# A two-layer metaformer block: area attention with more of its second channel half in the prologue, its last result by halves, and its variance two steps earlier

## The chip, the cores and the metric

The kernel runs on one core of one Trainium2 chip. A core has five engines, each with a queue of its own that it works off in order: TensorE (PE in the profile, with its weight loads as PEld), VectorE (DVE), ScalarE (ACT), GpSimd (POOL) and SyncE (SP, which here only issues DMA). The metric is the device time of one launch in microseconds (us).

## The reference, cut to what matters

Two layers work on x of shape (2, 256, 64, 64). The first layer adds area attention and then an LSTM over tokens; the second adds a mixer with a state-space part and then a layer of experts. The change touches only the area attention:

```python
x = x + _L0_conv_ref(_ln_c(x), ...)      # _ln_c: normalise over the 256 channels
# in _L0_conv_ref, after batch norms folded into scales:
qk, vv = 1x1 projections of the normalised x
pp = 5x5 depthwise convolution of vv, padded by 2
# 8 areas: 2 images x 4 bands of 16 rows (1024 positions each); 8 heads of 32
attn = softmax(q . k / sqrt(32))          # inside one area
o = attn . v
return 1x1 projection of (o + pp)
```

All of it is computed in float32.

## The kernel before, in words

The function `area_attention` (line 94) runs 16 groups, two for each of the 8 areas: group G is area A = G // 2 and channel half c = G % 2, that is four heads. A group has 16 steps. Step t takes query half n = t // 8 (512 queries) and key block m = t % 8 (128 keys). The loop over all 256 steps stands at the end of the function. The order of instructions on each engine is the order in which the source issues them (`manual_schedule`), and the tables in the source say which piece of side work is issued in which step.

One step issues, in this order:

- `scores` (line 347): for each head a small bf16 matmul that puts the negated row maxima into PSUM (line 352) and the float32 matmul of key and query on top (line 357); then ACT makes the exponentials (line 364) into two tiles `ex`. There are three buffers of each `ex` tile for even m, one for odd m.
- `values` (line 374) of the step before: weights times V, summed over the 8 steps in the bank `av_o` (line 370).
- work from a table SMALL: `place` (line 290) turns the row maxima of a later half on PE (line 294), copies them on ACT (line 298, `rows`) and spreads them with four small DMAs on SP (line 301).
- `maxima` (line 265): the scores of a later group, transposed in role (line 270), and DVE's maximum over them (line 275). This is how the row maxima of the softmax are known before its exponentials.
- one addition of two `ex` tiles on POOL (line 577), a part of the softmax's sums. A dependency written by hand ties it to the DVE operation before the maxima and to the last matmul of the maxima, so that it runs beside the reductions.
- a number of taps of the convolution on DVE (line 324), from the tables TAPS and TAPS_FIRST; an area has 50, the two first ones of line 313 included.
- work from the tables MINE/FIRST and AROUND: projections (`query`, `key`, `v_half`, `output`, all through line 166), averages over channels (`mean`, `variance`, line 178) and transposes of V (`v_tokens`, line 239). Most of them use the one PSUM bank `po`, which ACT empties.
- `sums` (line 385) two steps after each fourth step: the sums on PE, then after every second half DVE's division (lines 397 to 405).
- work from LATE and LATE_AROUND: `join` (line 280, row maxima in three bf16 parts), `centre` (line 187), `square`, `root` (lines 199 to 206: a transpose on DVE, an addition and a power on POOL, a transpose back on DVE), `scale`, `add_taps` (line 332), `residual` (line 345).

`scores` and `maxima` share the PSUM tiles `ps` of two banks each; there are three of them, so that a tile can be written when the one three places before it was emptied. There is one buffer `xn` of normalised x.

An entry `(k, f, ...)` in MINE means f for group G + k; in AROUND it means f for area A + k. So `(1, variance, 0)` in AROUND[0] at step 6 is the variance of the next area, first half, in step 6 of every even group. Area 0 has tables of its own, for both of its groups.

Before the loop stands a prologue for area 0: mean, centring, variance, root and scaling by halves (the generator `norm`), then query, key, eight `maxima`, V, `join` and `place`. After the loop: the last additions, the last `sums`, `add_taps` and the output of the last area in four projections, each of 512 positions by 128 channels, and two residual additions of 1024 positions.

The next stage, the LSTM's `recurrence`, starts with small loads of weights for the mixers (`bc_rest`, `taps`, `w_xdt`, `w_dtp`, `w_in`), a copy `w_dt` on DVE (line 1120), and transposes of x on PE (line 693).

Of the kernel before, what the change touches and what calls it, by code (L numbers as in the profile page):

```python
# [18 lines left out]
P = 128  # L19
# [74 lines left out]
def area_attention(tc, sh, ap):  # L94
# [13 lines left out]
    with ExitStack() as ctx:  # L108
# [42 lines left out]
        def bank():  # L151
            return ps2.tile([P, 512], F32, name="po", tag="po")
# [78 lines left out]
        def v_tokens(A, c, half):  # L231

            blocks = bank().rearrange("p (m d) -> p m d", d=P)
            src = vhs[A][:, c, 2 : 2 + AROWS].rearrange("p r w -> p (r w)")
            if half == 0:
                vts[A, c] = p2.tile([P, NM, P], F32, name="vt")
            for m in range(HM):
                at = (half * HM + m) * P
                nc.tensor.transpose(blocks[:, m], src[:, at : at + P], sh.ident)
            nc.scalar.copy(vts[A, c][:, half * HM : half * HM + HM], blocks)  # L240

        def rows_of(wt, G, half, name, s, t):
            A, c = GROUPS[G]
            ps = bank()
            project(wt, c, columns(xns[A]), half, ps)
            out = p2.tile([P, 512], F32, name=f"{name}{half}")
            nc.scalar.activation(out, ps, AF.Identity, scale=s[:, c : c + 1], bias=t[:, c : c + 1])
            return out

        def query(G, half):  # L250
            if half == 0:
                nms[G] = p3.tile([P, NQ, GH, NM], F32, name="nm")
            qs[G, half] = rows_of(w["wq"], G, half, "q", s_qk, t_qk)

        def key(G, half):
            ks[G, half] = rows_of(w["wk"], G, half, "k", s_qk[:, 2:4], t_qk[:, 2:4])

        def head(h):
            return slice(HD * h, HD * h + HD)
# [149 lines left out]
        with ExitStack() as own:  # L409
            early[0] = own.enter_context(tc.tile_pool(name="a_early", bufs=1))  # L410
            def fold(name, k):
                cols = sh.prm[:, COL[name]].rearrange("p (f k) -> p f k", k=k)
                return bn_fold(nc, cp, sh.eps5, *(cols[:, f] for f in range(4)), name)

            s_qk, t_qk = fold("qk", 4)
            s_v, t_v = fold("v", 2)
            for half in range(2):
                mean(0, half)

            def norm(at, half):  # L420
                for c in range(2):
                    centre(0, c, at)
                    square(0, c, at)
                yield
                variance(0, half)
                yield
                root(0, 0, at)
                root(0, 1, at)
                yield
                for c in range(2):  # L430
                    scale(0, c, at)
                yield

            first, second = (norm(at, half) for half, at in enumerate(HALVES))
            next(first)
            next(first)
            next(second)
            for _ in first:
                pass
            query(0, 0)  # L440
            key(0, 0)
            next(second)
            maxima(0, 0)
            next(second)
            maxima(0, 1)
            next(second)
            maxima(0, 2)
            key(0, 1)
            maxima(0, 3)
            s_pe, t_pe = fold("pe", 2)  # L450
            s_pr, t_pr = fold("pr", 2)

            nc.scalar.activation(p1.tile([P, 1], F32, name="idle"), sh.eps5, AF.Exp)

            w_pe = cp.tile([P, 2, 25], F32, name="w_pe")
            for c in range(2):
                every = sh.prm[:, COL["w_pe"]].rearrange("p (c k) -> p c k", c=2)
                nc.vector.tensor_scalar(w_pe[:, c], every[:, c], s_pe[:, c : c + 1], None, ALU.mult)
            for at, works in enumerate([
                [(0, 0), (0, 1)], [(1, 0)], [(1, 1)], [],  # L460
            ]):
                maxima(0, at + 4)
                for c, half in works:
                    v_half(0, c, half)
            join(0, 0, nc.vector)
            place(0, 0)
            for half in range(2):
                v_tokens(0, 0, half)
            early[0] = None
        pe = ctx.enter_context(tc.tile_pool(name="a_ex", bufs=1))  # L470

# [5 lines left out]
        LATE = {5: [(1, join, 0)], 13: [(1, join, 1)]}  # L477
        AROUND = [
            {
                2: [(0, v_tokens, 1, 0)], 3: [(0, v_tokens, 1, 1)], 4: [(-1, output, 0, 0)],  # L480
                6: [(1, variance, 0)], 7: [(1, variance, 1)], 8: [(-1, output, 0, 1)],
                10: [(-1, output, 1, 0)], 14: [(1, v_half, 0, 0)],
            },
            {
# [5 lines left out]
        LATE_AROUND = [  # L490
            {
                0: [(1, centre, 0)], 1: [(1, square, 0)], 2: [(1, centre, 1), (-1, add_taps, 1)],
                3: [(1, square, 1)], 7: [(1, root, 0)],
                8: [(1, root, 1), (1, scale, 0)], 9: [(-1, residual, 0)], 10: [(1, scale, 1)],
            },
            {7: [(-1, residual, 1)], 15: [(0, add_taps, 0)]},
        ]

        FIRST = [
            {  # L500
                0: [(0, query, 1)], 1: [(1, query, 0)], 2: [(1, key, 0)], 3: [(1, key, 1)],
                4: [(1, query, 1)], 14: [(2, query, 0)], 15: [(2, key, 0)],
            },
            {0: [(1, key, 1)], 2: [(1, query, 1)], 11: [(2, query, 0)], 12: [(2, key, 0)], 15: [(2, key, 1)]},
        ]
        SMALL_FIRST = [{5: [(0, place, 1)], 13: [(1, place, 0)]}, SMALL]
        LATE_FIRST = [{4: [(0, join, 1)], 9: [(1, join, 0)], 13: [(1, join, 1)]}, LATE]
        AROUND_FIRST = [
            {
                6: [(1, mean, 0)], 7: [(1, mean, 1)], 8: [(0, v_tokens, 1, 0)], 10: [(1, variance, 0)],  # L510
                11: [(1, variance, 1)], 12: [(0, v_tokens, 1, 1)],
            },
            {
                1: [(1, v_half, 0, 0)], 3: [(1, v_half, 1, 0)], 4: [(1, v_half, 0, 1)], 6: [(1, v_half, 1, 1)],
                7: [(1, v_tokens, 0, 0)], 8: [(1, v_tokens, 0, 1)], 10: [(2, mean, 0)], 14: [(2, mean, 1)],
            },
        ]
        LATE_AROUND_FIRST = [
            {
                7: [(1, centre, 0)], 8: [(1, centre, 1), (1, square, 0)], 9: [(1, square, 1)],  # L520
                11: [(1, root, 0)], 12: [(1, root, 1), (1, scale, 0)], 13: [(1, scale, 1)],
            },
            LATE_AROUND[1],
        ]


        AHEAD = {t: [(1, t + 2)] if t < 14 else [(2, t - 14)] for t in range(16)}
        order = [(0, 8 + i) for i in range(8)] + [(1, i) for i in range(16)]
        AHEAD_FIRST = [{}, {**AHEAD, 0: [(1, 0), (1, 1)], 1: [(1, 2), (1, 3)]}]
        for t in range(1, 14):  # L530
            AHEAD_FIRST[0][t] = [order.pop(0) for _ in range(2 if t < 12 else 1)]

        TAPS = [
            [1, 0, 0, 2, 2, 2, 2, 1, 0, 0, 1, 2, 2, 2, 3, 2],
            [2, 0, 2, 2, 3, 2, 2, 1, 1, 0, 3, 2, 3, 2, 2, 1],
        ]
        TAPS_FIRST = [
            [3] + [0] * 11 + [2, 2, 4, 4],
            [1, 1, 3, 2, 2, 2, 3, 2, 2, 2, 2, 3, 3, 2, 3, 2],
        ]  # L540

        def works(G, t, *tables):
# [12 lines left out]
        for g in range(16 * len(GROUPS)):  # L555
            G, t = divmod(g, 16)
            A, c = GROUPS[G]
            n, m = divmod(t, NM)
            new = A == 0
            if t == 0 and c == 0:  # L560
                conv = taps(A)
            exs = scores(G, n, m)
            if pending is not None:
                values(*pending)
            works(G, t, SMALL_FIRST[c] if new else SMALL, {})

            mm, before = None, latest[0]
            for k, at in (AHEAD_FIRST[c] if new else AHEAD).get(t, ()):
                if G + k < len(GROUPS):
                    mm = maxima(G + k, at)  # L570
            pair = None
# [4 lines left out]
            if pair is not None:  # L576
                add = nc.gpsimd.tensor_tensor(pair[0], *pair, ALU.add)  # L577
                if mm is not None:
                    tc.add_manual_dep(add.ins, mm.name, at_end, reason="beside the reductions")
                    tc.add_manual_dep(add.ins, before.name, at_end, reason="beside the reductions")  # L580
            for _ in range((TAPS_FIRST if new else TAPS)[c][t]):
                next(conv, None)
            works(G, t, FIRST[c] if new else MINE, (AROUND_FIRST if new else AROUND)[c])
            if g in due:
                sums(*due.pop(g))
            works(G, t, LATE_FIRST[c] if new else LATE, (LATE_AROUND_FIRST if new else LATE_AROUND)[c])
            pending = G, n, m, exs
            if m % 2:
                odd = exs[1]
                if m % 4 == 3:  # L590
                    due[g + 2] = G, n, m // 4, pairs
                    pairs = pairs[-1:]
            else:
                pairs = (pairs if m % 4 else []) + [exs]
        nc.gpsimd.tensor_tensor(pairs[-1][1], pairs[-1][1], odd, ALU.add)
        values(*pending)
        for g in sorted(due):
            sums(*due[g])
        last = len(AREAS) - 1
        add_taps(last, 1)  # L600
        for co in range(2):
            for half in range(2):
                output(last, co, half)
            residual(last, co)


def root_steps(nc, pool, v, shape, eps, name="ir"):
# [1655 lines left out]
```

## Time and profile before

| what | us |
|---|---|
| median of 3 runs (lowest, highest) | 3035.14 (3035.07, 3035.3) |
| the profiled execution | 3031.56 |
| its span, first to last instruction | 3029.7 |
| prologue of attention, to the loop's first bias matmul | 69.85 |
| groups 0 and 1 (area 0) | 114.33, 106.04 |
| groups 2 to 13 | 1056.20 |
| groups 14 and 15 and what follows, to the last residual addition | 184.55 |
| all later stages | 1498.73 |
| PE busy in the span | 2738.2 (90%) |
| DVE busy | 2181.1 (72%) |
| ACT busy | 1347.7 (44%) |
| POOL busy | 1358.4 (45%) |

The stretches are cut by time: a group begins with the first matmul of line 352 in its first step. Lines of the profile name the engine, the source line, the operation, the tile written and the tiles read, the size, the number of instructions merged in the row, and in square brackets the idle time before them and what ended it. Row times are start and length in us from the span's start. A projection of 128 x 512 in float32 shows as four matmul passes.

### The profile page before, as it was taken

How to read it: one execution, taken by the hardware profiler on the slowest of the kernel's cores; microseconds unless marked ns; L12 is line 12 of the kernel's file. 1: busy time of each engine (PE TensorE's matmuls, PEld its weight loads, DVE VectorE, ACT ScalarE, POOL GpSimd, SP SyncE). 2: the span in 40 equal slices, each digit the busy share in tenths (PEclk: the TensorE clock that was granted, in tenths of full speed). 3: DMA queues.
4: the chain of work that ended last, by engine and by line, in shares of the span. 5: the costliest groups of instructions: out<-in, count | busy, mean ns of one | idle time of the engine just before them, and what ended most of it. 6: DMA issues, size and time to landing. Idle time of an engine off the chain costs nothing. (4 is left out here: it accounts for less than half of the span.)

```text
span 3029.7 us, 45443 instructions
## 1 busy us (share of the span) xinstructions
PE 2738.2 (90%) x17798; PEld 1519.2 (50%) x17798; DVE 2181.1 (72%) x3224; ACT 1347.7 (44%) x2417; POOL 1358.4 (45%) x1037
## 2 busy tenths in 40 slices
PE   6989999999999999998789999978887589999994
PEld 2222232332323233222179999963444478888882
DVE  4689999999989999898956676679988812222115
ACT  2334454554544454444444455557653822222223
POOL 1354545544454554545623000028773156666651
PEclk8999999999999999999889999989999789999995
DMA  3000000000000000000024000005552446666658
GB/s 126 1 1 1 1 1 1 1 1 1 1 1 1 1 1 1 2 1 1 5 87 161 2 1 1 2 12 153 146 145 64 159 164 228 227 226 227 227 189 337
DMA packets 58658, 220.33 MB, mean 73 GB/s; under 512 B 14440, under 2 KB 15344, under 8 KB 48704
## 3 DMA queue, kind: packets, MB, share of 16 engines
q0 software_dynamic: 25440, 125.24, 11.6%
q1 hardware_dynamic: 31760, 87.82, 9.0%
q10 hardware_dynamic: 1232, 4.25, 0.4%
q8 instruction: 142, 2.33, 0.3%
q14 instruction: 84, 0.69, 0.1%
HBM read 173.30 MB, written 43.58 MB: 72 GB/s over the span
## 5 line engine op out<-in xcount | busy, mean ns | idle before, releaser
L577 POOL TENSOR_TENSOR ex<-ex,ex 128x1024 f32<-128x1024 f32 x255 | 614.5, 2412 | 645.3 <-PE ps L270 287.5
L275 DVE TENSOR_REDUCE nm<-ps 128x2 f32<-128x1024 f32 x512 | 601.0, 1218 | 102.4 <-PE ps L270 101.6
L364 ACT ACTIVATE ex<-ps 128x1024 f32<-128x1024 f32 x512 | 497.9, 1022 | 308.2 <-PE ps L357 269.3
L324 DVE SCALAR_TENSOR_TENSOR acc<-vh,w_pe,acc 128x1008 f32<-128x1008 f32 (+7 forms) x384 | 553.0, 1442 | 7.1
L270 PE MATMUL ps<-k,q 32*128 32x512 f32 x2048 | 347.7, 644 | 13.1 <-DVE nm L275 13.1
L2007 DVE COPY xt<-px 128x512 f32<-128x512 f32 x68 | 47.0, 691 | 397.7 <-PE px L2005 397.7
L2019 ACT ACTIVATE act<-ph,wt 128x256 f32<-128x256 f32 x272 | 128.8, 474 | 396.0 <-PE ph L2017 391.9
L2017 PE MATMUL ph<-xt,wt 128*128 128x256 f32 x1088 | 293.2, 393 | 3.3 <-ACT act L2019 1.7
L357 PE MATMUL ps<-q,k 32*128 32x512 f32 x2048 | 285.0, 607 | 0.0
L370 PE MATMUL av_o<-ex,vt 128*32 128x512 f32 x2048 | 278.0, 609 | 4.8 <-ACT ex L364 4.6
L2027 PE MATMUL py<-wt,act 128*128 128x256 f32 x1088 | 279.6, 380 | 0.0
L270 PEld LDWEIGHTS ps<-k,q 32*128 32x128 f32 x2048 | 123.1, 184 | 216.1 <-issue 75.0
L2017 PEld LDWEIGHTS ph<-xt,wt 128*128 128x128 f32 x1088 | 191.6, 192 | 66.4 <-DVE xt L2007 23.4
L774 PE MATMUL z<-xs,u 128*128 128x128 f32 x1872 | 222.2, 275 | 0.4 <-ACT xs L754 0.4
L774 PEld LDWEIGHTS z<-xs,u 128*128 128x128 f32 x1872 | 215.7, 192 | 0.6 <-ACT xs L754 0.6
L2027 PEld LDWEIGHTS py<-wt,act 128*128 128x128 f32 x1088 | 202.2, 191 | 25.0
L798 ACT ACTIVATE t<-z,bias 128x128 f32<-128x128 f32 x468 | 136.3, 361 | 144.5 <-PE z L786 144.4
L2042 POOL DMA_INDIRECT results<-y,ri x136 | 138.0, 1015 | 139.4 <-DVE y L2035 98.3
L786 PE MATMUL z<-xs,v 128*128 128x128 f32 x1512 | 180.1, 275 | 0.1
L786 PEld LDWEIGHTS z<-xs,v 128*128 128x128 f32 x1512 | 174.3, 192 | 0.7 <-DVE xs L805 0.7
L1508 POOL TENSOR_TENSOR cs<-hs,cs 128x1024 f32<-128x1024 f32 x63 | 148.7, 2363 | 54.1 <-DVE hs L1501 32.7
L370 PE MATMUL po<-ex,ones 128*32 128x512 f32 x1024 | 136.6, 638 | 37.0 <-ACT rows L298 25.7
(408 smaller groups left out, 3809.9 us busy)
## 6 DMA issues: line engine op xcount, KB each, us to landing
cs<-c_rows SPq DMA_DIRECT2D x128, 256.0 KB
y<-results SPq DMA_DIRECT2D x32, 512.0 KB
x<-xrows SPq DMA_DIRECT2D x8, 1024.0 KB
rows<-xt SPq DMA_DIRECT2D x16, 512.0 KB
out_x<-res POOLq DMA_DIRECT2D x15, 512.0 KB, 7.1
xrows<-xn SPq DMA_DIRECT2D x24, 256.0 KB
x<-in_x SPq DMA_DIRECT2D x4, 1024.0 KB
x<-in_x ACTq DMA_DIRECT2D x4, 1024.0 KB
```

What stands on the lines that cost most here:

```text
L270: mm = nc.tensor.matmul(tiles[h // 2][:, h % 2], qs[G, i // HM][head(h), i % HM * P : (i % HM + 1) * P], ks[G, n][head(h)], start=True, st ...
L275: nc.vector.tensor_reduce(nms[G][:, n, 2 * j : 2 * j + 2, i], tiles[j], AX.X, ALU.max, negate=True)
L324: mark(nc.vector.scalar_tensor_tensor(part, vh[:, c, 2 + r0 + dy : 2 + r1 + dy, w0 + dx : w1 + dx], w_pe[:, c, k : k + 1], part, ALU.mult, ...
L357: nc.tensor.matmul(tiles[h // 2][:, h % 2], k[head(h), m % HM * P : (m % HM + 1) * P], qs[G, n][head(h)], start=False, stop=True, tile_pos ...
L364: nc.scalar.activation(exs[i], tiles[i], AF.Exp, scale=HD**-0.5)
L370: nc.tensor.matmul(to[head(h)], lhs, exs[h // 2][:, h % 2], start=first, stop=last, tile_position=(0, HD * h))
L577: add = nc.gpsimd.tensor_tensor(pair[0], *pair, ALU.add)
L774: nc.tensor.matmul(z[c][:, g, :m], u[:, k, c, g], xt[:, k], start=g == GATES[0] and k == 0, stop=False, skip_group_check=True,)
L786: nc.tensor.matmul(z[c][:, g, :m], v[:, k, c, g], h[:, k], start=False, stop=k == 1, skip_group_check=True,)
L1508: nc.gpsimd.tensor_tensor(now["c", n], hs, now["c", n], ALU.mult)
L2017: nc.tensor.matmul(ph[:, hc], wt[:, at : at + P], xt[:, c], start=c == 0, stop=c == 1)
L2027: nc.tensor.matmul(py[:, j], act[:, hc, j * P : j * P + P], wt[:, at : at + C], start=hc == 0, stop=hc == NH - 1,)
```

## The change

Five things are done.

1. In the prologue, area 1's mean is issued after the first variance; query(0,0) and key(0,0) go into `ps` tiles instead of the bank `po`; the second root part is issued one piece later. query(0,1), query(1,0) and key(1,0) are issued before the loop.
2. Group 0 has tables of its own; group 1 uses the general ones. Steps 0 to 9 of group 0 hold two `maxima`, steps 10 to 15 one; group 1 has one in every step. Area 0's taps are 13 in group 0 and 37 in group 1 (before 15 and 35).
3. In even groups, the next area's variance is issued in steps 4 and 6 (before 6 and 7), the first root part in step 6 (before 7), and the previous area's first output half in step 7 (before 4).
4. After the loop, the last area's output is made by halves of 512 positions: the half of y that is complete is added to the convolution, projected and added to x before the last `sums` are issued; then the other half. Both projections of a half use the two banks of one `ps` tile.
5. `rows_of`, `query` and `key` take the PSUM tile as an argument.

```diff
-        def rows_of(wt, G, half, name, s, t):
+        def rows_of(wt, G, half, name, s, t, ps):
             A, c = GROUPS[G]
-            ps = bank()
+            ps = bank() if ps is None else ps
...
             next(first)
             next(first)
             next(second)
+
+            for half in range(2):
+                mean(1, half)
             for _ in first:
                 pass
-            query(0, 0)
-            key(0, 0)
+            query(0, 0, wide()[:, 0])
+            key(0, 0, wide()[:, 0])
             next(second)
             maxima(0, 0)
             next(second)
             maxima(0, 1)
-            next(second)
             maxima(0, 2)
+            for _ in second:
+                pass
+            maxima(0, 3)
             key(0, 1)
-            maxima(0, 3)
...
-            for at, works in enumerate([
-                [(0, 0), (0, 1)], [(1, 0)], [(1, 1)], [],
-            ]):
+            for at in range(4):
                 maxima(0, at + 4)
-                for c, half in works:
-                    v_half(0, c, half)
+                v_half(0, *divmod(at, 2))
+            for half in range(2):
+                v_tokens(0, 0, half)
+            query(0, 1, wide()[:, 0])
             join(0, 0, nc.vector)
             place(0, 0)
-            for half in range(2):
-                v_tokens(0, 0, half)
+            query(1, 0, wide()[:, 0])
+            key(1, 0, wide()[:, 0])
...
         AROUND = [
             {
-                2: [(0, v_tokens, 1, 0)], 3: [(0, v_tokens, 1, 1)], 4: [(-1, output, 0, 0)],
-                6: [(1, variance, 0)], 7: [(1, variance, 1)], 8: [(-1, output, 0, 1)],
+                2: [(0, v_tokens, 1, 0)], 3: [(0, v_tokens, 1, 1)], 4: [(1, variance, 0)],
+                6: [(1, variance, 1)], 7: [(-1, output, 0, 0)], 8: [(-1, output, 0, 1)],
...
-                3: [(1, square, 1)], 7: [(1, root, 0)],
+                3: [(1, square, 1)], 6: [(1, root, 0)],
...
+        FIRST = {
+            0: [(1, key, 1)], 1: [(1, query, 1)], 11: [(2, query, 0)], 12: [(2, key, 0)], 15: [(2, key, 1)],
+        }
+        SMALL_FIRST = {5: [(0, place, 1)], 9: [(1, place, 0)]}
+        LATE_FIRST = {3: [(0, join, 1)], 7: [(1, join, 0)], 13: [(1, join, 1)]}
+        LATE_AROUND_FIRST = {
+            1: [(1, centre, 0)], 2: [(1, centre, 1), (1, square, 0)], 3: [(1, square, 1)],
+            6: [(1, root, 0)], 8: [(1, root, 1), (1, scale, 0)], 9: [(1, scale, 1)],
+        }
...
-        AHEAD_FIRST = [{}, {**AHEAD, 0: [(1, 0), (1, 1)], 1: [(1, 2), (1, 3)]}]
-        for t in range(1, 14):
-            AHEAD_FIRST[0][t] = [order.pop(0) for _ in range(2 if t < 12 else 1)]
+        AHEAD_FIRST = dict(AHEAD)
+        for t in range(14):
+            AHEAD_FIRST[t] = [order.pop(0) for _ in range(2 if t < 10 else 1)]
...
         TAPS_FIRST = [
-            [3] + [0] * 11 + [2, 2, 4, 4],
-            [1, 1, 3, 2, 2, 2, 3, 2, 2, 2, 2, 3, 3, 2, 3, 2],
+            [0] * 10 + [1, 2, 3, 2, 3, 2],
+            [2, 0, 2, 2, 3, 3, 3, 2, 2, 0, 3, 3, 3, 3, 3, 3],
         ]
...
-            new = A == 0
+            new = G == 0
...
-        for g in sorted(due):
-            sums(*due[g])
         last = len(AREAS) - 1
-        add_taps(last, 1)
-        for co in range(2):
-            for half in range(2):
-                output(last, co, half)
-            residual(last, co)
+        acc = accs.pop((last, 1)).rearrange("p r w -> p (r w)")
+        for half, at in enumerate(HALVES):
+            if half == 1:
+                for g in sorted(due):
+                    sums(*due[g])
+            y = ys[last, 1][:, at]
+            nc.vector.tensor_tensor(y, y, acc[:, at], ALU.add)
+            ps = wide()
+            for co in range(2):
+                project(w["wpr"], co, lambda k: ys[last, k], half, ps[:, co])
+                o = p2.tile([P, 512], F32, name="o_last", tag=f"q{half}")
+                nc.scalar.activation(
+                    o, ps[:, co], AF.Identity, scale=s_pr[:, co : co + 1], bias=t_pr[:, co : co + 1]
+                )
+                to = area(last)[:, co, at]
+                nc.vector.tensor_tensor(to, to, o, ALU.add)
```

More of the change, by code (lines that the diff above doesn't have):

```diff
@@ L248, in rows_of, with query, key @@
             return out
-        def query(G, half):
+        def query(G, half, ps=None):
             if half == 0:
                 nms[G] = p3.tile([P, NQ, GH, NM], F32, name="nm")
-            qs[G, half] = rows_of(w["wq"], G, half, "q", s_qk, t_qk)
-        def key(G, half):
-            ks[G, half] = rows_of(w["wk"], G, half, "k", s_qk[:, 2:4], t_qk[:, 2:4])
+            qs[G, half] = rows_of(w["wq"], G, half, "q", s_qk, t_qk, ps)
+        def key(G, half, ps=None):
+            ks[G, half] = rows_of(w["wk"], G, half, "k", s_qk[:, 2:4], t_qk[:, 2:4], ps)
         def head(h):
@@ L427, in norm @@
                 root(0, 0, at)
+                yield
                 root(0, 1, at)
-                yield
                 for c in range(2):
@@ L497, in area_attention @@
         ]
[L499 to L524, printed above, removed]
+        FIRST = {
[7 more added lines that the diff above has]
+        }
         AHEAD = {t: [(1, t + 2)] if t < 14 else [(2, t - 14)] for t in range(16)}
         order = [(0, 8 + i) for i in range(8)] + [(1, i) for i in range(16)]
-        AHEAD_FIRST = [{}, {**AHEAD, 0: [(1, 0), (1, 1)], 1: [(1, 2), (1, 3)]}]
-        for t in range(1, 14):
-            AHEAD_FIRST[0][t] = [order.pop(0) for _ in range(2 if t < 12 else 1)]
+        AHEAD_FIRST = dict(AHEAD)
+        for t in range(14):
+            AHEAD_FIRST[t] = [order.pop(0) for _ in range(2 if t < 10 else 1)]
         TAPS = [
@@ L564, in area_attention @@
                 values(*pending)
-            works(G, t, SMALL_FIRST[c] if new else SMALL, {})
+            works(G, t, SMALL_FIRST if new else SMALL, {})
             mm, before = None, latest[0]
-            for k, at in (AHEAD_FIRST[c] if new else AHEAD).get(t, ()):
+            for k, at in (AHEAD_FIRST if new else AHEAD).get(t, ()):
                 if G + k < len(GROUPS):
@@ L580, in area_attention @@
                     tc.add_manual_dep(add.ins, before.name, at_end, reason="beside the reductions")
-            for _ in range((TAPS_FIRST if new else TAPS)[c][t]):
+            for _ in range((TAPS_FIRST if A == 0 else TAPS)[c][t]):
                 next(conv, None)
-            works(G, t, FIRST[c] if new else MINE, (AROUND_FIRST if new else AROUND)[c])
+            works(G, t, FIRST if new else MINE, AROUND[c])
             if g in due:
                 sums(*due.pop(g))
-            works(G, t, LATE_FIRST[c] if new else LATE, (LATE_AROUND_FIRST if new else LATE_AROUND)[c])
+            works(G, t, LATE_FIRST if new else LATE, LATE_AROUND_FIRST if new else LATE_AROUND[c])
             pending = G, n, m, exs
```

## The prediction

> **What bounds the kernel now.** I read the busy time by stage first (stretches cut at the first bias matmul, line 352, of each step or group), then the instructions in order of time at the places that the diff touches. The page's chain of waits lies almost wholly in the last stage and says nothing here. Stretches of the attention stage, each as start:end, length, then busy time of PE, PEld, DVE, ACT, POOL with counts, clock, DMA share, GB/s: the prologue, groups 0 and 1, an even group (4), an odd one (3), and the end.
>
> ```profile
> 0.00:69.85 69.85, 42.63 (x118) 14.31 (x119) 33.05 (x57) 14.34 (x24) 10.71 (x18) 0.86 0.36 136
> 69.85:184.18 114.33, 107.71 (x607) 33.24 (x606) 77.44 (x70) 42.79 (x51) 44.76 (x29) 0.95 0.01 1
> 184.18:290.22 106.04, 95.89 (x584) 29.69 (x584) 96.27 (x84) 43.57 (x52) 43.61 (x29) 0.94 0.00 1
> 382.08:467.93 85.85, 84.39 (x564) 26.64 (x564) 83.12 (x75) 42.00 (x50) 41.59 (x27) 1.00 0.01 2
> 467.93:557.98 90.05, 85.65 (x565) 26.77 (x565) 81.75 (x75) 44.01 (x52) 47.59 (x29) 0.98 0.00 1
> 1489.78:1530.97 41.19, 23.43 (x66) 6.52 (x62) 24.32 (x29) 6.69 (x9) 7.63 (x5) 0.67 0.03 8
> ```
>
> The steady groups have PE and DVE both nearly full (84.4 and 83.1 of 85.85), so a gain there can only be a stall that goes. The slack is in the prologue and the end, and even groups are some 4 to 5 us longer than odd ones. Group 4 shows why (in order of time):
>
> ```profile
> 513.23 5.46 POOL L203 TENSOR_TENSOR root<-root,minus_half 128x32 f32<-128x32 f32 x1
> 518.65 2.34 POOL L577 TENSOR_TENSOR ex<-ex,ex 128x1024 f32<-128x1024 f32 x1
> 521.03 1.02 ACT L364 ACTIVATE ex<-ps 128x1024 f32<-128x1024 f32 x1 [3.50 <-POOL ex L577]
> 522.25 3.31 PE L370 MATMUL po<-ex,ones 128*32 128x512 f32 x16 [3.54 <-ACT rows L298]
> ```
>
> POOL's power holds its queue 5.46 us; step 8's pair addition comes late; step 9's second exponential waits for that (the odd `ex` tile has one buffer); behind it on ACT stands `rows` of `place`; PE's sums need the one `po` bank that `rows` empties. Step 9 takes 10.35 us (515.15 to 525.50) instead of the 6.07 of group 3.
>
> **Prologue: gain 9.3.** The projections in it are latency-bound and cold:
>
> ```profile
> 22.08 3.75 PE L166 MATMUL po<-xn,wq 128*128 128x512 f32 x4 [6.35 <-issue]
> 26.70 3.69 PE L166 MATMUL po<-xn,wk 128*128 128x512 f32 x4 [0.87 <-ACT q L247]
> 31.26 1.98 PE L178 MATMUL po<-sq,mean_w 128*128 128x512 f32 x4 [0.87 <-ACT k L247]
> ```
>
> Area 1's mean (2 x 1.98, two copies of 0.58) goes into PE's idle 15.7 to 22.1; area 1's x is there by 11.7 (its bytes in the DMA record). The Trainium skill ("TensorE: Matmul & The Clock Gate", Part 1) says that about 3.4 us of activity releases the clock and an idle window of that length throttles it. The row agrees for the idle 6.35 (3.75 for what takes 1.98 warm). With the gaps down to about 1 us the rule gives 1.98 each for query and key; if they stayed cold, as in the row, the sum loses 3.5. I take warm. Key no longer waits for query's copy, being in another bank: query 22.1-24.0, key 24.0-25.7, copy 26.5, variance 25.5-27.3, first reduction 28.5 (now 34.35). DVE then does 2 reductions, a transpose 31.6, 4 reductions to 36.3 (POOL's root hides under these; before, DVE idled for it from 37.3 to 40.8), transpose and two scalings 38.3, 2 reductions 40.6. PE: second key 37.7-39.5, copy 40.4, then four rounds of maxima and `v_half`, PE-bound at 3.0 each, to 52.4; vh copy 53.2; two token transposes with copies 55.7; query(0,1) to 56.9; `place`; rows on ACT at 58.0, behind q's copy. Before, rows ended at 67.28 and line 357 began at 71.62, 4.3 later, waiting for the four small DMAs on SP; so now 62.3. query(1,0) and key(1,0), 3.8 of PE, fit into these 4.3.
>
> **Groups 0 and 1: gain 15.7.** Five projections (area 1's mean twice, query(0,1), query(1,0), key(1,0)) leave the loop, and 10 steps instead of 13 hold two maxima; the `mx` loads on SP are as many as before and queue behind nothing. A step with two maxima and a projection stays 7.61 (three PSUM buffers, which ACT and DVE must empty; its plain PE work is 6.6), with transposes 6.3, with neither 5.7. Step 0 ends at 62.3 + 5.4 + 1.9 = 69.6. Steps 1 to 9: 7.6 + 6.3 + 6.9 + 8.1 + 7.7 + 7.6 + 5.7 + 6.5 + 8.5 = 64.9; centring (1.2 twice) waits for query(1,1), the last reader of the one `xn` buffer, and costs about 0.6 in steps 3 and 4; the power ends in bare steps 7 to 8, where POOL has room. That is 134.5. From there DVE bounds. A tap costs 1.32: group 1's 96.27 less 18 pairs of reductions at 2.36, two sum ends of 3.03 and 1.5 of small work, over 35. Steps 10 to 15: 6 x 2.36 + 13 x 1.32 + 0.2 = 31.5; group 1, now 16 pairs and 37 taps: 37.8 + 48.8 + 6.1 + 1.5 = 94.2; 1 carried over. 126.7 at 97% busy (group 3's share) is 130.6, so group 2 begins at 265.1, not 290.2: 25.1 with the prologue.
>
> **Even groups 2 to 12: gain 2.4 each, 14.4.** Variance moves to steps 4 and 6 (squares end 489.3, its matmul at 491.8: no wait), output(-1,0,0) from 4 to 7; PE's work is the same. But `ln_t` cannot move a whole step: on DVE it stands behind step 6's two taps, which end at 507.99, so it runs 508.0-509.2 (before 511.5-512.7), power 509.8-515.2. Queued behind `ln_t` are step 7's reductions (1.3 later): PE waits 0.55 for a PSUM tile at step 8. Behind the power are now two additions, 515.2-517.6 and 517.6-519.9. Step 9 starts at 515.7; its second exponential 519.95, rows 521.2 (before 522.2), sums 521.25-523.2, warm after 1.5 idle, where they took 3.31. So step 9 ends at 523.2 against 525.5, and step 11 sheds 0.1. DVE's wait for the root (3.2) goes, but is off the path. Bounds: 0 if the additions come no earlier, 4.6 if even groups reach the odd ones' length. Group 14 has no variance; its output in step 7 fills a PE idle of 2.6: gain 1 (0 to 2).
>
> **The end: loss 3.6.** What is there now:
>
> ```profile
> 1505.59 1.22 DVE L332 TENSOR_TENSOR y<-y,acc 128x1024 f32<-128x1024 f32 x1
> 1506.60 0.27 SPq L1117 DMA_DIRECT2D w_dtp<-in_w_dtp  x1
> ...
> 1525.27 3.63 PE L166 MATMUL po<-y,wpr 128*128 128x512 f32 x4 [0.87 <-ACT o L339]
> 1529.75 1.22 DVE L345 TENSOR_TENSOR x<-x,o 128x1024 f32<-128x1024 f32 x1 [7.93 <-ACT o L339]
> 1531.51 2.89 PE L693 MATMUL turned<-ident,x 128*128 128x128 f32 x13 [2.61 <-DVE w_dt L1120]
> ```
>
> After: half 0's addition ends at 1507.5, co 0 projected by 1510.5, copied 1511.3. The second projection waits for this copy although it goes into another bank: both are one `wide` tile and the built program has the wait. co 1 to 1515.2; only then, in PE's order, the sums, to 1517.6; DVE's sum end and half addition, 3.9, to 1521.5; then projection, copy, projection, copy, addition: 1526.8 if PE is warm, 1529.5 if cold, against 1530.97. The same skill rule speaks for warm (gain 4.2); the rows speak for cold (PE stayed at 3.78 for 15 us with gaps of 0.87; gain 1.5). I take 2.6. Against it: the next stage's small loads (taps, w_xdt, w_dtp, bc_rest) are at present released by the last tap at 1505.6, and load under the end. In the changed program they wait for the last residual addition, on SP's queue behind the four w_in to w_out issues (0.6 each). From that addition: w_dtp issued at 3.1, landed about 5.5 (before, at most 2.9 after its issue), w_dt's matmul 6.2; bc_rest lands at 3.3, its eight DVE operations and b_conv (0.8) stand ahead of the w_dt copy, which ends at 6.8. PE's transposes wait for that copy: 0.54 before, 6.7 after. Loss 6.2 (5 to 7), and the recurrence behind it is serial. Other stages are unchanged.
>
> **Sum.** -25.1 - 14.4 - 1 + 3.6 = -36.9. The profiled execution had 3031.56 us (span 3029.7); so 2994.7. The runs' median, 3035.14, lies 3.6 above it: 2998.
>
> **Rivals.** (a) Even groups reach 85.8: they now average 90.4, so 6 x 4.6 instead of 14.4, 2985. For it: the power is out of step 8; against: the taps ahead of `ln_t`. (b) The shift gives nothing, since two additions now queue behind the power: 3012. (c) The moved projections free PE, but groups 0 and 1 keep to DVE's pace and its gaps (busy 91% in group 1 before): 126.7 / 0.91 adds 9, 3007. (d) Slower: `ln_t` ahead of step 7's reductions starves the PSUM ring, so that every even group loses a step. Priced at 0.55 above; from 3.7 per group it eats all the rest (22.5 / 6). One step of 5.35 in six groups ends at 3045. Against it: step 7 has one tap, and DVE catches up in it.
>
> **How the numbers follow.** Main case 0.55; (a) 0.15, (b) 0.15, (c) 0.10, (d) 0.05. The main case alone spans 2991 to 3005 (clock in the prologue 3.5, end -2 to +3, even groups 1.5 to 3 each). With (a) and (b): 2982 to 3014. About 0.2% (6 us) is what a measurement of this kernel can tell from no change; only (d) is on the other side: faster 0.94, same 0.02, slower 0.04.
>
> **What would show it.** First matmul of line 357 at 62 to 63; group 2's start near 265; group 1 DVE-bound with 37 taps; even groups near 87.6, step 9 near 7.5, power starting 3 to 4 us earlier relative to its step; transposes of the next stage 6 to 7 us after the last addition. Wrong if even groups do not change or pass 90, or group 2 starts after 275.

## The result and the profile after

The changed kernel takes 3006.3 us (median of 3 runs, 3005.05 to 3007.19) against 3035.14: ratio 0.9908, 95% interval 0.9894 to 0.9922. Run twice more, unaltered, it took 3004.1 and 3005.8 us; ratios 0.9893 (0.9877 to 0.9909) and 0.9876 (0.9860 to 0.9892) to the kernel before on the same chips (3039.1, 3042.6). So it is 0.9 to 1.2% faster, 29 to 37 us. The prediction, 2998 (2982 to 3014), was right as a whole, with all three medians 6 to 8 us above its middle. Not every term of it was right.

The stretches of the changed kernel by time: prologue, groups 0, 1, 2, an odd group (3), an even one (4), step 8 of group 0, the end from group 15's last step to the last residual addition. Below, warm and cold mean that the same row of PE is short or long: a projection of four passes takes 1.98 us warm and up to 3.78 cold. Columns as before: start:end, length, busy time of PE, PEld, DVE, ACT, POOL, granted clock, DMA share, GB/s.

```profile
0.00:62.65 62.65, 48.07 (x137) 16.69 (x138) 30.07 (x54) 17.54 (x29) 10.70 (x18) 0.95 0.39 152
62.65:175.12 112.47, 104.57 (x611) 32.03 (x611) 84.84 (x76) 42.09 (x49) 43.75 (x31) 0.94 0.00 1
175.12:265.97 90.85, 84.84 (x560) 26.10 (x560) 88.11 (x80) 41.41 (x49) 40.76 (x26) 0.98 0.00 1
265.97:360.78 94.81, 88.35 (x564) 27.22 (x564) 84.82 (x78) 44.02 (x52) 49.19 (x29) 0.96 0.00 1
360.78:446.90 86.12, 84.66 (x564) 26.67 (x565) 83.41 (x76) 41.98 (x50) 42.02 (x27) 1.00 0.01 2
446.90:536.44 89.54, 86.25 (x563) 27.06 (x563) 80.66 (x74) 44.02 (x52) 48.04 (x29) 0.98 0.00 1
122.18:131.96 9.78, 8.81 (x38) 2.53 (x36) 6.81 (x6) 2.52 (x3) 5.31 (x6) 0.65 0.01 2
1462.21:1498.01 35.80, 17.70 (x64) 5.00 (x60) 22.90 (x22) 6.70 (x9) 5.55 (x2) 0.77 0.00 0
```

In the prologue PE is now busy 48.07 of 62.65 us (42.63 of 69.85 before), in groups 0 and 1 together 189.4 of 203.3 (203.6 of 220.4): the projections that left the loop stand where PE used to idle. No run undoes this part of the change alone, so its gain rests on these stretches.

The even group is only 0.5 us shorter than before, and the granted clock falls to 0.65 in one step in the middle of work. The table therefore has three traces of the same program: the gain per stretch, in us, against the one trace of before.

| stretch | predicted | first trace | second | third |
|---|---|---|---|---|
| to the first matmul of line 357 (71.6 before) | 9.3 | 7.4 | 7.7 | 5.4 |
| from there to group 2 | 15.7 | 16.8 | 18.1 | 21.1 |
| group 2 (91.86 before) | 2.4 | -2.95 | -0.1 | -0.1 |
| groups 3 to 13 | 12 | 5.5 | 8.4 | 8.3 |
| group 14 | 1 | 1.7 | 1.7 | 1.7 |
| group 15 to the next stage's transposes | -3.6 | -2.45 | -2.5 | -2.7 |
| sum up to there | 36.9 | 26.0 | 33.3 | 33.8 |
| all later stages (1498.2 before), code unchanged | 0 | 0.4 | -4.9 | -10.1 |

The later stages alone took 1497.8 to 1512.5 us in the traces of this study. Each has the same 8804 matmuls there; PE is busy for 1324.9 us in the shortest and 1342.3 in the longest, VectorE for 831.7 and 833.2. A single trace or a median of few runs therefore doesn't show a gain of 5 us; the stretches do, where the cause is visible in them.

Where the even group still loses time, in order of time in group 4:

```profile
488.41 5.46 POOL L203 TENSOR_TENSOR root<-root,minus_half 128x32 f32<-128x32 f32 x1
493.83 2.36 POOL L564 TENSOR_TENSOR ex<-ex,ex 128x1024 f32<-128x1024 f32 x1
...
495.97 1.30 DVE L212 TENSOR_TENSOR xn<-xn,ln_r 128x1024 f32<-128x1024 f32 x1
496.15 3.32 POOL L564 TENSOR_TENSOR ex<-ex,ex 128x1024 f32<-128x1024 f32 x1
...
499.50 1.02 ACT L364 ACTIVATE ex<-ps 128x1024 f32<-128x1024 f32 x1 [2.26 <-POOL ex L564]
500.42 0.24 ACT L298 CAST rows<-po 48x128 bf16<-48x128 f32 x1
...
500.72 2.50 PE L370 MATMUL po<-ex,ones 128*32 128x512 f32 x16 [2.29 <-ACT rows L298]
```

The power starts 3.6 us earlier relative to its step, as forecast. But the second addition behind it takes 3.32 us, not 2.35, beside VectorE's scaling (line 212); the second exponential, the row copy and the sums follow it. PE stands still for 2.29 us (3.54 before).

And the hand-off to the next stage, in order of time:

```profile
1497.32 0.69 DVE L601 TENSOR_TENSOR x<-x,o_last 128x512 f32<-128x512 f32 x1 [3.96 <-ACT o_last L597]
1498.08 0.57 SPq L1091 DMA_DIRECT2D w_in<-in_w_in  x1
...
1501.05 0.43 SPq L1104 DMA_DIRECT2D taps<-in_c_rows  x1
...
1501.91 0.28 SPq L1114 DMA_DIRECT2D w_dtp<-in_w_dtp  x1
...
1505.10 0.29 DVE L1117 COPY w_dt<-w_dt 128x128 f32<-128x128 f32 x1 [0.95 <-PE w_dt L1116]
1505.45 4.76 PE L690 MATMUL turned<-ident,x 128*128 128x128 f32 x24 [0.38 <-DVE w_dt L1117]
```

All loads stand behind the last addition, which ends at 1498.01; the transposes follow 7.4 us later (0.5 before).

### The profile page after: what moved, and what is told of

It reads as the page before. It is cut to its first block, busy times and chain, and to the rows that moved or that the text cites. A ratio compares the mean times of both kernels' runs of the same rounds, so it can differ in the third digit from the quotient of the medians.

```text
span 3003.3 us, 45441 instructions
## 1 busy us (share of the span) xinstructions
PE 2724.1 (91%) x17798; PEld 1514.7 (50%) x17798; DVE 2173.3 (72%) x3227; ACT 1348.0 (45%) x2417; POOL 1357.7 (45%) x1037
## 5 line engine op out<-in xcount | busy, mean ns | idle before, releaser
L352 PE MATMUL ps<-mx,ones_b 3*128 3x512 bf16 x1024 | 132.5, 386 | 37.2 <-DVE nm L275 35.0
```

## Experiments

All start from the changed kernel. Places at the end are counted from the start of group 15 and written with a plus sign. Of the single edits, only the undone shift of the variance (ratio 0.9947 to the kernel before, 0.9930 to 0.9963) is told from the changed kernel (0.9876 to 0.9908) by its times. The others (0.9862 to 0.9927) are read from their stretches.

**The same program again.**

> The changed kernel itself, unaltered, as a second draw beside the others. In four of the variants so far the stretches that they share with it came out differently from run to run, with PE's granted clock: area 0 from the first bias matmul to group 2 in 199.1 to 203.3 us, an even group in 88.2 or in 89.4 to 89.8. Theory: these are two lengths of the same instructions, warm and cold, so the median lies within 4 us of 3006 but single times spread over 10 us or more; step 4, 8 and 9 of group 0 take either 8.2, 6.9, 8.8 or 9.8, 9.8, 10.5. Rival: the variants differ because their code differs; then this run repeats 112.5 for group 0 and 89 to 90 for the even groups.

3004.1 us (3002.16 to 3011.73). Group 0 took 110.75, the even groups 4 to 12 88.16 to 88.19 and once 89.35. So the rival, that other lengths come from other code, falls. The third trace had group 0 at 107.82. Its stretches: group 0, its step 8, group 4.

```profile
64.69:172.51 107.82, 100.00 (x613) 30.92 (x613) 84.74 (x76) 41.89 (x49) 43.82 (x31) 0.98 0.01 1
122.64:129.53 6.89, 5.82 (x36) 1.65 (x36) 6.79 (x6) 2.42 (x3) 5.33 (x6) 1.00 0.01 2
441.82:529.99 88.17, 84.88 (x563) 26.81 (x562) 80.46 (x74) 44.05 (x52) 48.07 (x29) 1.00 0.00 1
```

Step 8 of group 0 takes 6.89 us at clock 1.00 here and 9.78 at 0.65 in the first trace, with the same work on VectorE (6.8). The two lengths belong to one program.

**The even groups: the shift undone, and one instruction moved.**

The tables in short form:

```diff
 # e2: tables of even groups from 2 on
-    4: variance(1,0)  6: variance(1,1), root(1,0)  7: output(-1,0,0)
+    4: output(-1,0,0)  6: variance(1,0)  7: variance(1,1), root(1,0)
 # e3: even groups from 2 on, ahead of the sums of step 9
-    8: root(1,1), scale(1,0)
+    8: root(1,1)    9: scale(1,0)
```

> The changed kernel with variance, first root part and output in steps 6, 7, 7 and 4 of the even groups from 2 on, as before (area 0 keeps its new tables). Theory: the shift by itself gains about 1 us in each even group, through step 9 alone (8.3 to 9.9 us now, 10.3 before), so the even groups 4 to 12 come back to about 90.1 on average from 89.0, and the time rises by 5 to 7 us, to about 3012. Rival 1: the shift gives nothing, because two additions queue behind the power and one of them takes 3.3 us; then no change within 1.5 us. Rival 2: the shift gives the 2.4 per group of the prediction and another part of the change took it back: 3020.

3019.9 us. Even groups 4 to 12: 90.07 on average, as before the change (90.11). Over the eight traces that have the shift and no other edit of these groups, 40 such groups average 88.54 (29 of 88.2 and 11 of 89.3 to 89.8; group 8 is among the long ones in all eight). So the shift gains about 1.55 per group, not 0 and not 2.4. The time itself fell on the second rival's 3020, by more than I expected. The stretches account for 11 us, in six groups and in group 14, which I had left out (78.76 again); the other 3 to 5 lie within the spread of area 0 and the later stages. The number is no support for that rival: with the shift undone these groups are as before, so no other part of the change took anything from them.

> The changed kernel with the first scaling of the even groups from 2 on issued in step 9, ahead of the sums, instead of step 8. Theory: the second addition behind the power takes 3.32 us instead of 2.35 because the scaling on VectorE (two operands in SBUF) runs beside it; without that it takes 2.4, the second exponential of step 9 and the row copy come 1.0 sooner, PE waits 1.3 instead of 2.3 us for the sums and stays warm, and step 9 takes 7 to 7.9 us instead of 8.3 to 9.9: 1 to 2 us per even group, the time falls by 6 to 12, to about 2998. Rival: the length of step 9 is set by the order on ScalarE and by the one bank, not by the length of the addition; then even groups keep 88.2 to 89.8 and the time is 3006 within 2.

2998.4 us. The three additions behind the power, first in group 4 of the changed kernel, then in group 6 of this one:

```profile
493.83 7.95 POOL L564 TENSOR_TENSOR ex<-ex,ex 128x1024 f32<-128x1024 f32 x3
```

```profile
664.75 7.10 POOL L565 TENSOR_TENSOR ex<-ex,ex 128x1024 f32<-128x1024 f32 x3
...
669.44 1.02 ACT L364 ACTIVATE ex<-ps 128x1024 f32<-128x1024 f32 x1 [1.28 <-POOL ex L565]
670.36 0.25 ACT L298 CAST rows<-po 48x128 bf16<-48x128 f32 x1
...
670.66 1.06 PE L370 MATMUL po<-ex,ones 128*32 128x512 f32 x8 [1.32 <-ACT rows L298]
671.02 1.91 DVE L212 TENSOR_TENSOR xn<-xn,ln_r 128x1024 f32<-128x1024 f32 x1
```

They take 7.10 us instead of 7.95; PE waits 1.32 instead of 2.29, and step 9 takes 7.3 instead of 8.3 where PE is warm. No addition of the even groups' steps 8 and 9 is longer than 2.38 now; instead the scaling takes 1.91, having started while the third addition ran. Ten such groups, from this run and the last one below, average 87.73: a gain of 2.4 on before. That is the 2.4 of the prediction, once the addition has the length that the prediction gave it. The rival falls.

**The row maxima a step later, too (on top of the moved scaling).**

```diff
-    SMALL = {1: place(0,1), 9: place(1,0)}
+    SMALL = {1: place(0,1), 10: place(1,0)}
```

> The changed kernel with the first scaling of the even groups in step 9 and, in all groups but the first, the row maxima of the next group placed in step 10 instead of step 9. Theory: what is left of the long step 9 is that the sums wait for the one bank, which the row copy empties only behind the second exponential; without it the sums start with the end of the second addition, 1.2 us sooner, PE is idle under 1 us, and step 9 takes 6.0 to 6.3, the even groups 86 to 86.4 (87.4 with the scaling moved alone, 88.2 in the changed kernel). Time 3006 - 6 x 2 = 2994. Rival: the second exponential itself is what PE waits for, since step 10's scores need its PSUM tile; then step 9 stays at 7.3 and the time at 2998.

3000.5 us. Step 9 takes 5.90, as the theory has it, but step 11 grows from 5.67 to 7.01, so the even groups stay at 87.3 (86 to 86.4 expected, and 2994). In order of time in group 4:

```profile
501.07 2.09 DVE L212 TENSOR_TENSOR xn<-xn,ln_r 128x1024 f32<-128x1024 f32 x1
...
506.25 1.22 DVE L345 TENSOR_TENSOR x<-x,o 128x1024 f32<-128x1024 f32 x1
...
507.38 2.35 DVE L275 TENSOR_REDUCE nm<-ps 128x2 f32<-128x1024 f32 x2
...
508.66 0.39 PE L352 MATMUL ps<-mx,ones_b 3*128 3x512 bf16 x2 [1.32 <-DVE nm L275]
```

The wait went to VectorE: scaling, sum end and residual addition now stand ahead of step 10's reductions with no pause of PE to hide them. In groups 1 and 2 the later place was no gain: they took 93.3 and 94.2, against 91.3 and 91.9 in the third trace, whose group 0 is as short. Part of that is the clock (step 1 of group 2 has 8.98 at 0.81, against 7.35 at 1.00).

**The end and the hand-off.**

```diff
 # e4: last outputs in the tile o
-    o = p2.tile([P, 512], F32, name="o_last", tag=f"q{half}")
+    both = p1.tile([P, NA], F32, name="o_last", tag="o")   # once per half
+    o = both[:, HALVES[co]]
 # e8: e4, and a PSUM tile for each projection
-    ps = wide()                # once per half
+    ps = wide()[:, 0]          # once per co
 # e1, e11: the end of the kernel before
```

> The changed kernel with the four last outputs in the tile o (as the kernel before had them) instead of two tiles that share the buffers of the queries. Theory: the small loads of the next stage go where those query buffers lie and so wait for the last residual addition; with the outputs in o they are released by the last reader of the convolution, load under the end, and the transposes follow the last addition after 0.5 to 1 us instead of 7.4. The time falls by 6 to 7 us, to about 2999.5. Rival: the loads' place makes no difference, because they stand behind the four large loads on SyncE; then no change within 1 us.

3001.6 us. In order of time:

```profile
1469.59 0.36 SPq L1105 DMA_DIRECT2D taps<-in_c_rows  x1
...
1470.39 0.27 SPq L1115 DMA_DIRECT2D w_dtp<-in_w_dtp  x1
...
1489.61 0.69 DVE L602 TENSOR_TENSOR x<-x,o_last 128x512 f32<-128x512 f32 x1 [3.96 <-ACT o_last L598]
...
1490.51 0.29 DVE L1118 COPY w_dt<-w_dt 128x128 f32<-128x128 f32 x1 [0.21 <-PE w_dt L1117]
...
1490.86 2.00 PE L691 MATMUL turned<-ident,x 128*128 128x128 f32 x8 [0.44 <-DVE w_dt L1118]
```

The loads go out 20 us ahead of the last addition, and the transposes follow it after 0.56 us. The edit changes nothing but the buffer of `o_last`, so what delayed them was its place in the queries' buffers. That the next stage's small tiles lie there is inferred; no trace shows addresses. The time fell by 2.5 to 4.7, not by the 6 to 7 expected, which is less than single runs of one program differ.

> The changed kernel with the last outputs in the tile o and with a PSUM tile of its own for each of the four last projections. Theory: the second projection of a half no longer waits for the copy of the first (0.87 us plus the copy), so the last residual addition comes 1.6 us sooner, 99.7 us after the start of group 15 instead of 101.4 with a warm PE, and the next stage's transposes 0.6 later; together 8.5 us: 2998. Rival: the wait comes from ScalarE, which copies one after the other in any case; then the addition stays at 101.4 and only the hand-off is gained: 2999.5.

3000.1 us. In order of time:

```profile
1486.80 2.84 PE L166 MATMUL ps<-y,wpr 128*128 128x512 f32 x6 [3.07 <-DVE y L592]
...
1490.49 0.69 DVE L602 TENSOR_TENSOR x<-x,o_last 128x512 f32<-128x512 f32 x1 [1.03 <-ACT o_last L598]
```

The passes of both projections run as one row, without the pause for the copy; the rival falls. The last addition ends at +97.4 instead of +101.35, and the transposes come at +97.9 instead of +108.8. The gain is more than the 1.6 I expected, because in the changed kernel the projection behind the pause ran cold (3.78 us), and here both of the second half are warm. The times show 4 us less than the changed kernel's 3004.1 on the same chip, not 10.9; the later stages of this trace took 1507.3.

> The changed kernel with the end of the kernel before (sums first, whole-area addition of the convolution, four projections through the one bank, two residual additions of 1024 positions). Theory: the new end reaches its last residual addition 4.4 us sooner (101.4 from the start of group 15 against 105.8), but makes the next stage wait 7.4 us instead of 0.5 for its first transposes; so with the old end the transposes come 106.3 us after the start of group 15 instead of 108.8, and the time falls by 2.5 us, to about 3003.8. Rival: the hand-off is no loss of its own, because the next stage is held by something else anyway; then the old end is 4.4 us slower, 3010.7.

3012.0 us (2995.01 to 3015.24), though the trace has the transposes at +102.8, 6 us sooner than in the changed kernel. But that trace is of the fastest of the five executions, 2995.01; the other four took 3010 and more. Hence a second trial:

> The changed kernel with the old end once more, because the first trial of it contradicts itself: its trace has the next stage's transposes 102.8 us after the start of group 15 (108.8 in the changed kernel), while the median of its times, 3012, is above the changed kernel's 3004 to 3006. Theory: the old end has two lengths, 102.3 when PE turns warm in it and 105.8 when it stays cold, and both beat 108.8 with the hand-off added, so beside the changed kernel on the same chip this one is 2 to 6 us faster, 2999 to 3003; the earlier median came from the clock in the other stages, which the single trace missed. Rival: the old end costs more than the trace shows, and this one is again 5 us or more above the changed kernel.

> The changed kernel unaltered, beside the one with the old end. Expected as in its other runs: 3003 to 3006, group 0 in 107.8, 110.8 or 112.5, even groups 88.2 or 89.4 to 89.8, the hand-off 7.4 to 7.6, the last addition 101.3 or 103.6 after the start of group 15. Theory: above the kernel with the old end by 2 to 6 us. Rival: below it by 5.

3005.82 (2995.66 to 3015.01) with the old end, 3005.81 (3000.43 to 3007.8) with the new one. The rival falls (not 5 us slower) and the theory isn't confirmed in the times: the transposes come at +102.8 and +109.0 again, but the times of the old end spread over 20 us, and the later stages took 1512.5 and 1508.3. The two traces of the old end are 20 us apart, and none of it is in the end (the last addition at +102.26 and +102.25): 9.5 lie ahead of it, mostly in groups 0 and 2, and 10.5 in the later stages. Whether the 6 us reach the end of the program stays open.

**Taps.**

```diff
-    TAPS_FIRST = [[0]*10 + [1,2,3,2,3,2], [2,0,2,2,3,3,3,2,2,0,3,3,3,3,3,3]]
+    TAPS_FIRST = [[2,1,0,1,1,1,1,0,0,0,1,2,3,2,3,2], [2,0,2,2,3,2,2,1,1,0,3,2,3,2,3,2]]
```

> The changed kernel with 7 of the 37 taps of group 1 issued in steps 0 to 6 of group 0 (20 and 30 taps). Theory: from step 10 of group 0 VectorE sets the pace and carries a backlog into group 2, whose steps 0 and 1 take 7.0 and 7.4 (8.9 cold) instead of 5.4; in steps 0 to 9 PE sets it and VectorE idles about 2.9 us per step. Seven taps of 1.32 are 9.2 us off VectorE; group 1 falls from 91 to about 86 and group 2 from 91.9 to about 88.5, 6 to 9 us together, group 0 stays within 1: about 2999. Rival: the taps delay the reductions of group 0's doubled maxima, PE waits for PSUM tiles there, and group 0 grows by as much as group 1 sheds: 3006.

2999.8 us. Its groups 1 and 2:

```profile
175.00:261.21 86.21, 82.79 (x559) 26.02 (x559) 81.71 (x74) 41.34 (x49) 41.18 (x26) 1.00 0.01 1
261.21:353.03 91.82, 87.03 (x563) 27.04 (x563) 83.20 (x77) 44.04 (x52) 49.20 (x29) 0.98 0.01 1
```

Group 1 falls to 86.2 from 90.9 or 91.3, and group 2's first two steps to 12.7 (as before the change) from 15.9 or 14.4, in the first and the second trace; no step of group 0 is longer than in a trace without the taps, so the rival falls. Together 6.8 to 7.8, as expected: VectorE set the pace there, and part of its backlog was paid in group 2. Group 2 as a whole is still 91.8, because its step 9 ran cold here (9.88 instead of 8.28).

**All together.**

> All of the moves together: scaling in step 9, row maxima placed in step 10, seven taps moved to group 0, the last outputs in o with a PSUM tile for each projection. Theory: the gains add, since they lie in different stretches: 7 us in area 0 and group 2, 0.8 us in each of six even groups, 10.9 us at the end and the hand-off, 22 us below the changed kernel's 3004 to 3006: 2983. Rival: the row maxima in step 10 make PE wait in step 11 (7.0 us there, 5.7 in the changed kernel) and that costs more where VectorE is behind, in groups 1 and 2, so that the taps' gain is lost: 2990.

> The same without the move of the row maxima (placed in step 9 as in the changed kernel). Theory: even groups 87.4 when warm, as in both single experiments, but step 9 has 1.3 us of idle PE and runs cold in some groups (88.7), so 2983 to 2986. Rival, as for the run beside it: without the wait of step 11 groups 1 and 2 keep the taps' gain, and this one is the faster of the two by 3 to 5 us.

2985.4 and 2981.4 us, ratios to the kernel before 0.9842 (0.9826 to 0.9858) and 0.9838 (0.9816 to 0.9861); both are faster than either kernel. The second is 23 to 25 us below the changed kernel's medians, but only 11 to 21 by the ratios, since the kernel before was faster on this chip too (3034.4). In its stretches the gains add: against the second trace groups 1 and 2 are 6.1 shorter, the even groups 4 to 12 together 4.1, and the end and hand-off 10.9; group 0, warm here, is 2.9 shorter, and the prologue, with a cold second mean, 4.5 longer. Group 2 takes 89.44, 2.4 less than before. The rival about groups 1 and 2 isn't borne out in the stretches (86.2 and 89.45 with the later place, 87.7 and 89.44 without). The median without it is lower by the 4 us that the rival named, but the two are not told apart by their times.

## Why the prediction was right, and where it was not

Of the signs it named, the start of group 2 near 265 and the power 3 to 4 us earlier came true. Line 357 at 62 to 63, even groups near 87.6 and step 9 near 7.5 (8.3 warm, up to 9.9 cold) did not, and the hand-off was 7.4 to 7.7, not 6 to 7.

**Prologue, 9.3: 7.4, and 5.4 to 7.7 over three traces.** Query and key are warm, as taken; the step that failed is "second key 37.7-39.5". In order of time:

```profile
22.20 1.98 PE L166 MATMUL ps<-xn,wq 128*128 128x512 f32 x4 [0.98 <-DVE xn L212]
24.02 1.88 PE L166 MATMUL ps<-xn,wk 128*128 128x512 f32 x4
...
37.69 3.66 PE L166 MATMUL po<-xn,wk 128*128 128x512 f32 x4 [0.49 <-DVE xn L212]
```

It took 3.35 to 3.75 in all 13 traces of kernels with this prologue. PE had no long pause ahead of it, but in the first trace the maxima before it ran at a clock of 0.64 already (33.00 to 37.69; 1.00 from 27.60 to 33.00). In six of the 13 the second mean was cold as well (3.78 for 1.98), which moved what follows by up to 2. Over the 13 traces line 357 begins at 63.7 to 69.5: a gain of 2.1 to 8.0, so 9.3 lies beyond the best of them.

**Groups 0 and 1, 15.7: 16.8 to 21.1.** The 64.9 for steps 1 to 9 was 65.8 in the third trace and 72.0 in the first, through steps 4, 8 and 9 alone. From step 10 VectorE set the pace as forecast (busy 97% of group 1). What the step left out is the backlog that group 2 pays; the taps' experiment shows it. Group 2 began at 263.8 to 266.0, as forecast (265.1), but by luck: the prologue gained less than reckoned and these groups more.

**Even groups, 2.4 each: about 1.55.** This is the failed step: "Behind the power are now two additions, 515.2-517.6 and 517.6-519.9". The second took 3.32, since the scaling that I had left on VectorE at that time runs beside it. I had the addition's price from rows where VectorE does reductions. The other price stood in the trace of before, where 18 additions that begin beside a tap or a residual addition take 3.16 to 3.39:

```profile
1490.97 5.68 DVE L324 SCALAR_TENSOR_TENSOR acc<-vh,w_pe,acc 128x945 f32<-128x945 f32 x3
1492.37 3.27 POOL L577 TENSOR_TENSOR ex<-ex,ex 128x1024 f32<-128x1024 f32 x1 [6.89 <-PE av_o L370]
```

Moving the scaling restored the 2.4. Of the rivals, (b) is excluded by the undone shift, (a) by 88.5 against 85.8, (d) by PE's extra wait at step 8, 0.40 (0.55 forecast), and (c) by group 1's 97%.

**Group 14, 1: 1.7. The end, -3.6: -2.5.** In the first trace the addition came 4.45 earlier (1.5 to 4.2 forecast, 2.6 taken) and the hand-off lost 6.9 (6.2). In three other traces with this end the addition came some 2 us later still (+103.5 to +103.8 for +101.35). That the second projection waits for the copy of the first, and for the one tile, is shown. But the comparison was with a cold end: the old end ran warm in both later traces and ended at +102.3, so beside it the new one gains 0.9 at the addition, and the end as a whole loses 6.0 rather than 2.5.

**From profile to median.** The prediction carried over 3.6 us from the profiled execution to the median; here it was 1.25. So the profiled execution missed by 10.4 (3005.05 for 2994.7) and the median by 8.3: 2.4 of the miss went away by luck. In the first trace groups 3 to 13 fell short by 6.5, group 2 by 5.4 and the prologue by 1.9; groups 0 and 1, group 14 and the end gave back 3. In the other two traces the sum is short by only 3.6 and 3.1, and the later stages are longer by 4.9 and 10.1. Of this the mis-sized step is about 5, six groups of 0.85; the rest lies in stretches that differ between traces of one program.

## What to carry to other kernels

Work that is timed to run beside certain instructions of another engine loses that when a long operation ahead of it is moved: price the neighbours anew, not only the queue. A new tile's place in memory decides when the next stage may load; look who reads that memory last. And before a few us are explained, run the same program again and compare the stretches at their granted clocks.

## What was not expected of the hardware

Some instructions of GpSimd and VectorE hold each other up for their whole length. In group 0 of the changed kernel, in order of time:

```profile
124.31 2.35 POOL L564 TENSOR_TENSOR ex<-ex,ex 128x1024 f32<-128x1024 f32 x1
124.51 2.19 DVE L285 TENSOR_TENSOR rest<-nm 128x16 f32<-128x16 f32 x1
```

The small operation, which reads two slices of `nm` (0.17 us at 480.77 in group 4), ends 0.04 after the addition. The Trainium skill ("SBUF — State Buffer", section "SBUF: two separate sides") says that a VectorE instruction with two SBUF inputs and a GpSimd one that reads SBUF exclude each other, and that the first to start keeps the shared ports to its end. The addition of 3.32 agrees: the scaling before it ends at 497.27, and 2.35 from there is 499.62, against 499.47. So do the rows of VectorE's reductions with their one input: beside them the addition keeps its 2.35. This rule spoke against an addition beside the scaling, and I had not weighed it.

PE's clock fell without a long pause. Before step 8 of group 0 PE was busy 5.60 of 5.76 us at clock 1.00; in step 8 it first waited 0.74 us for VectorE, in the first trace and in the third, and the clock of the step was 0.65 in the one and 1.00 in the other. The idle window of about 3.4 us, by which the prediction reckons, is thus not the only way to a low clock here. No run shows what decides it.
